# z and r gates of two of four batches by seven products over 64 partitions, two at a time on the halves of the array

## The chip, the cores and the metric

The kernel runs on one core of a Trainium2 chip. The metric is the device time of one execution in microseconds (us); of several runs the median is given. All arithmetic is float32.

## The reference, cut to what matters

Two layers work on 16 batches of 1024 nodes with 128 features; `adj` is a 1024 x 1024 matrix. The second layer takes nearly all of the time: a gated recurrent step, five times.

```
x = layernorm(x + adj @ (x @ weight) + bias)          # layer 0
h = x
for step in range(5):                                  # layer 1
    m  = adj @ h                                       # in_matrix == out_matrix == adj
    av = concat([m, m])
    u3 = h @ u3_w.T + u3_b
    z  = sigmoid(av @ w3_w.T + w3_b + u3)
    r  = sigmoid(av @ w4_w.T + w4_b + u3)
    hv = tanh(av @ w5_w.T + w5_b + (r * h) @ u5_w.T + u5_b)
    h  = (1 - z) * h + z * hv
out = layernorm(x + h)
```

Since both halves of `av` are the same, the kernel adds the two halves of w3, w4 and w5 once, at the start, and then works with 128 x 128 weights.

## The kernel before, in words

The batches go in four groups of four (`q`, 0 to 3; `QUAD` = 4), and each group makes five steps (`s`): 20 steps in the loop at L845. All instructions are written out by this Python code; the framework then orders each engine's queue by the written order and by what is ready, except that everything under `in_order` (L492, `tc.keep_in_program_order`) keeps its written order on its engine. All gate matmuls are under it, so TensorE's order in the gates is the one that the code spells out. The four engines that matter are TensorE (PE), VectorE (DVE), ScalarE (ACT) and the DMA queue of SyncE (SP).

**Adjacency products** (`aggregate`, L417). The product of adj with the state of four batches is made by a seven-product form (Winograd's) at two levels. The outer level pairs batches 0 and 1 with batches 2 and 3; `chain` (L358) makes the outer products 1 and 2, then 3, then 6 and 7, then 5 and 4, each by seven inner products in the order 1, 5, 6, 2, 7, 3, 4. The results of an inner product lie in the PSUM banks pa, pb and pc, and are emptied by ScalarE copies (L382 to L385 and L388) and VectorE additions (L386 and L387) into `first`, `rows` and `agg`. At the end L453 to L457 add the last pieces together in `agg` (features on partitions, nodes along the free axis), quarter after quarter: L455 for the second half of the nodes of each batch, L457 for the first half of batches 2 and 3. The first half of the nodes of batches 0 and 1 is ready in `agg` long before. `hooks` puts other work between inner products.

**Gates.** A unit is one batch `k` and one half `h` of its nodes (512 columns): eight units a step. A unit takes five matmuls of 128 x 128 weights on 512 columns: u3 on h (`gate_first`, L501; its result is copied by ScalarE, L509, into a second bank, so that r and z each have a seed to add to), w4 (`gate_r`, L519), w3 (`gate_z`, L534), w5 (L542) and u5 on r*h (L543). ScalarE makes the sigmoids (L522, L537) and the tanh (L553), VectorE r*h (`gate_rh`, L529) and the update in three operations: hv - h, times z, plus h (L558 to L560). The units are interleaved (L913 to L917): u3 of unit u, then w5 and u5 of unit u-3, then w4 and w3 of unit u-1. At a step's end `gates_begin` (L925) runs u3 of the next step's first three units. r of unit 0 and z of unit 0 are hooked into the last adjacency chain.

**Turning the state.** The next step needs the state with nodes on partitions. `turn_rows` (L577) transposes 32 x 32 blocks on VectorE and writes them to DRAM by an SP DMA; `fetch_rows` (L590) reads them back into `rows` with four DMAs for each batch. The first inner sums of the next step (`first_sums`, L317 to L320) are put between the updates of batch 3. In the last step of a group the state goes to `closing`, and the layernorm of a finished batch (`close`) is hooked into the adjacency chains of the next group.

**PSUM** has eight banks: a, c, g0, g1, g2 by tags, and pb and two `seeded` ones standing. `z_of` and `rh_of` are parts of `tsum`.

Of the kernel before, what the change touches and what calls it, by code (L numbers as in the profile page):

```python
# [15 lines left out]
STEPS = 5  # L16
QUAD = 4
# [3 lines left out]
def kernel(  # L21
# [62 lines left out]
    turned = [dram.tile([16, P, 64], F32, name=f"turned{i}") for i in range(3)]  # L84
# [67 lines left out]
    e12 = const.tile([P, 2, 4, 2, QT], F32, name="e12")  # L152
# [7 lines left out]
    for n in outer:  # L160
        e = extra[n]
        left[n] = {
            1: quarter(n, 0, 0), 2: quarter(n, 0, 1), 3: e[:, 2], 4: quarter(n, 1, 1),
            5: e[:, 0], 6: e[:, 1], 7: e[:, 3] if n < 3 else quarter(n, 1, 0),
        }
# [11 lines left out]
    def inner_left_12():  # L177
        a = [[blk[0][:, :, 2 * j : 2 * j + 2, ts(i, QT)] for j in range(2)] for i in range(2)]
        return left_sums(*a[0], *a[1], e12[:, :, 0], e12[:, :, 1], e12[:, :, 3], e12[:, :, 2])
# [33 lines left out]
    w_t = {n: const.tile([P, D], F32, name=f"{n}_t") for n in ("w3", "w4", "w5", "u3", "u5")}  # L213

# [16 lines left out]
    def layer1_weights():  # L231
# [5 lines left out]
        for w, raw in raw_of.values():  # L237
            if w.shape[1] == 2 * D:
                tc.keep_in_program_order(
                    nc.vector.tensor_add(raw[:, :D], raw[:, :D], raw[:, D : 2 * D])  # L240
                )

    def turn_weights():
        for name, (_, raw) in raw_of.items():
            pt = bank(f"pt_{name}")
            tc.keep_in_program_order(nc.tensor.transpose(pt[:, :P], raw[:, :D], ident))
            nc.vector.tensor_copy(w_t[name], pt[:, :P])
# [67 lines left out]
    def inner_sums(xs, dst):  # L315

        yield nc.vector.tensor_sub(dst[0], xs(0, 1), xs(0, 0))  # L317
        yield nc.vector.tensor_sub(dst[1], xs(1, 1), dst[0])
        yield nc.vector.tensor_sub(dst[2], xs(1, 1), xs(0, 1))
        yield nc.vector.tensor_sub(dst[3], xs(1, 0), dst[1])  # L320
# [96 lines left out]
    def aggregate(tag, src, hooks, turned=True):  # L417
# [34 lines left out]
        )  # L452
        for dst, a, b in ((0, p7, p4), (1, p7, p4), (2, p7, p5), (3, p7, p5)):  # L453
            cols = ts(dst % 2, HALF)
            nc.vector.tensor_add(agg[:, dst, HALF:], a[:, cols], b[:, cols])  # L455
            if dst >= 2:
# [40 lines left out]

    def gate_first(tag, u, part=None, seed=True):
        k, h = UNITS[u]
        pu = bank(f"pu_{tag}_{k}_{h}", part if part is None else part_of[part])  # L500
# [38 lines left out]
    def update_products(tag, k, h, part=None):  # L539
        cols = ts(h, HALF)  # L540
        ph = bank(f"ph_{tag}_{k}_{h}", part if part is None else part_of[part])
# [28 lines left out]

    def half_of(h):
        return (slice(None), 4) if h is None else (ts(h, HALF), 2)

    def between(k, h):
        return turned[k % 2] if h is None else turned[2][ts(h, 8)]

    def turn_rows(k, h=None, to=None):  # L577
        cols, n = half_of(h)
        to = between(k, h) if to is None else to
# [5 lines left out]
        tc.keep_in_program_order(nc.sync.dma_start(  # L585
            to.rearrange("g p x -> p g x"), t.rearrange("p (g x) -> p g x", x=64)
        ))
# [373 lines left out]
```

## Time and profile before

| what | value |
|---|---|
| median of 3 runs | 1768.44 us (1768.34 to 1768.82) |
| the profiled execution | 1769.02 us, span 1766.9 us |
| TensorE matmuls busy | 1755.7 us (99%) |
| TensorE weight loads busy | 1265.8 us (72%), beside the matmuls |
| VectorE busy | 1301.9 us (74%) |
| ScalarE busy | 800.0 us (45%) |
| one step (448.41 to 525.05 in the span) | 76.6 us |
| granted TensorE clock | 0.999 |

The profile is of one execution. A line of the page's groups or of the timeline names the source line (L519), the engine, the operation, what it writes and reads, the shape, the count, and in brackets how long the engine sat idle before it and what ended that. PEld is TensorE's weight load. A float32 matmul appears as two loads and two matmul instructions. The ends of matmuls are modelled, so their spacing is read from the starts.

### The profile page before, as it was taken

What the parts mean: (1) busy time and instruction counts of PE and PEld (TensorE: products, weight loads), DVE (VectorE), ACT (ScalarE), POOL (GpSimd) and SP (SyncE); (2) the same over time, 40 slices, a digit from 0 to 9 for tenths busy, and PEclk for the clock granted to TensorE, in tenths of its full rate; (3) what the DMA queues carried; (4) which work ended last, traced back from release to release, by engine and by line L of the source; (5) the groups of instructions that cost most, each with busy time, mean ns of one, the idle gap of its engine ahead of it and who ended that gap; (6) DMA issues with size and microseconds to landing.
All of it is one profiled execution on the core that took longest, in us unless ns stands there. A gap on an engine that the chain in (4) does not pass through costs nothing.

```text
span 1766.9 us, 19951 instructions
## 1 busy us (share of the span) xinstructions
PE 1755.7 (99%) x6709; PEld 1265.8 (72%) x6709; DVE 1301.9 (74%) x2286; ACT 800.0 (45%) x1424; POOL 103.3 (6%) x152
## 2 busy tenths in 40 slices
PE   9999999999999999999999999999999999999998
PEld 8988885766858577685867758586675857668584
DVE  7977777676766847777778667777778577777778
ACT  4355565334353434435354452535445353443537
POOL 1202220000000000000000000000000000000004
PEclk9999999999999999999999999999999999999999
DMA  8144354051423505143351424324243241514232
GB/s 276 49 143 144 120 137 107 20 119 26 94 60 72 143 12 133 46 120 68 87 131 56 112 57 99 85 71 119 55 113 99 57 93 27 131 25 107 60 84 95
DMA packets 405332, 161.34 MB, mean 91 GB/s; under 512 B 388336, under 2 KB 389488, under 8 KB 405232
## 3 DMA queue, kind: packets, MB, share of 16 engines
q1 hardware_dynamic: 402960, 153.01, 34.3%
q0 software_dynamic: 1696, 5.24, 1.1%
q10 hardware_dynamic: 576, 1.84, 0.3%
q8 instruction: 53, 0.87, 0.2%
q14 instruction: 47, 0.39, 0.1%
HBM read 93.98 MB, written 65.01 MB: 90 GB/s over the span
## 4 chain that ended last, share of the span: by engine, by line
PE 98%; DMA 1%; DVE 0%; POOL 0%; ACT 0%; issue 0%; POOLq 0%; SPq 0%; DVEq 0%; ACTq 0%
PE pb L398 25%; PE pc L398 14%; PE pa L398 14%; PE pu L519 8%; PE ph L542 8%; PE pu L501 8%; PE ph L543 8%; PE seeded L534 8%; PE pc_x L398 3%; PE pa_x L398 3%; PE seeded L475 2%; DMA hid<-in_adj_dram 1%; DMA agg<-in_adj_dram 0%; PE pt L633 0%; PE pt_end L836 0%; POOL rstd L265 0%
## 5 line engine op out<-in xcount | busy, mean ns | idle before, releaser
L398 PE MATMUL pb<-e,inner 128*128 128x256 f32 x864 | 206.2, 379 | 0.2 <-ACT pb L382 0.2
L558 DVE TENSOR_TENSOR tsum<-tsum,hid 128x512 f32<-128x512 f32 x158 | 108.7, 688 | 106.4 <-ACT tsum L553 106.3
L553 ACT ACTIVATE tsum<-ph,bh 128x512 f32<-128x512 f32 x158 | 108.5, 687 | 164.6 <-PE ph L543 164.5
L398 PEld LDWEIGHTS pb<-e,inner 128*128 128x128 f32 x864 | 167.7, 194 | 19.2 <-ACT pb L382 0.6
L519 PE MATMUL pu<-agg,w_t 128*128 128x512 f32 x320 | 163.7, 593 | 0.0
L542 PE MATMUL ph<-agg,w_t 128*128 128x512 f32 x320 | 163.4, 592 | 0.0
L543 PE MATMUL ph<-tsum,u_t 128*128 128x512 f32 x320 | 163.4, 592 | 0.0
L534 PE MATMUL seeded<-agg,w_t 128*128 128x512 f32 x320 | 163.4, 592 | 0.0
L501 PE MATMUL pu<-hid,u_t 128*128 128x512 f32 x320 | 157.0, 592 | 0.0
L522 ACT ACTIVATE tsum<-pu,br 128x512 f32<-128x512 f32 x160 | 110.1, 688 | 85.6 <-PE pu L519 85.6
L398 PE MATMUL pb<-s,inner 128*128 128x256 f32 x576 | 148.5, 380 | 0.0
L398 PE MATMUL pb<-a,inner 128*128 128x256 f32 x576 | 143.9, 379 | 0.0
L529 DVE TENSOR_TENSOR tsum<-tsum,hid 128x512 f32<-128x512 f32 x160 | 110.1, 688 | 37.9 <-ACT tsum L522 37.9
L398 PE MATMUL pc<-e,inner 128*128 128x256 f32 x560 | 133.9, 379 | 0.0
L398 PEld LDWEIGHTS pb<-s,inner 128*128 128x128 f32 x576 | 110.5, 194 | 24.8 <-issue 10.4
L537 ACT ACTIVATE tsum<-seeded,bz 128x512 f32<-128x512 f32 x160 | 110.0, 688 | 29.3 <-PE seeded L534 29.3
L398 PEld LDWEIGHTS pb<-a,inner 128*128 128x128 f32 x576 | 111.9, 194 | 12.4
L398 PEld LDWEIGHTS pc<-e,inner 128*128 128x128 f32 x560 | 109.2, 195 | 12.8 <-PE pu L501 0.7
L543 PEld LDWEIGHTS ph<-tsum,u_t 128*128 128x128 f32 x320 | 60.8, 190 | 76.5 <-issue 59.6
L542 PEld LDWEIGHTS ph<-agg,w_t 128*128 128x128 f32 x320 | 60.6, 190 | 75.1 <-issue 74.4
L501 PEld LDWEIGHTS pu<-hid,u_t 128*128 128x128 f32 x320 | 60.8, 190 | 73.5 <-issue 72.2
L559 DVE TENSOR_TENSOR tsum<-tsum 128x512 f32<-128x512 f32 x158 | 109.1, 691 | 4.9
(192 smaller groups left out, 2854.2 us busy)
## 6 DMA issues: line engine op xcount, KB each, us to landing
turned<-ypad SPq DMA_DIRECT2D x48, 512.0 KB, 3.8
rows<-turned SPq DMA_DIRECT2D x192, 128.0 KB, 2.9
hvs<-saved SPq DMA_DIRECT2D x24, 512.0 KB, 4.1
rows<-saved SPq DMA_DIRECT2D x20, 512.0 KB, 3.7
hid<-hidden SPq DMA_DIRECT2D x64, 128.0 KB, 3.4
turned<-ypad SPq DMA_DIRECT2D x32, 256.0 KB, 2.9
rows<-turned SPq DMA_DIRECT2D x128, 64.0 KB, 2.1
hidden<-ypad SPq DMA_DIRECT2D x12, 512.0 KB, 4.1
```

The costliest lines, as they stand in the source:

```text
L398: product = nc.tensor.matmul(bank_of[a][:, ts(o, QT)], chunk(a, o, c), left[n][a][:, c, :], start=(a in (1, 5) and o == 0 and c == 0), sto ...
L501: in_order(nc.tensor.matmul(pu, w_t["u3"], hid[:, k, ts(h, HALF)], start=True, stop=True, skip_group_check=True))
L519: in_order(nc.tensor.matmul(pu, w_t["w4"], agg[:, k, cols], start=False, stop=True, skip_group_check=True))
L522: pin(nc.scalar.activation(rh[:, cols], pu, AF.Sigmoid, bias=br))
L529: pin(nc.vector.tensor_mul(rh[:, cols], rh[:, cols], hid[:, k, cols]))
L534: in_order(nc.tensor.matmul(pz, w_t["w3"], agg[:, k, cols], start=False, stop=True, skip_group_check=True))
L537: pin(nc.scalar.activation(z_of[k % 2][:, cols], pz, AF.Sigmoid, bias=bz))
L542: in_order(nc.tensor.matmul(ph, w_t["w5"], agg[:, k, cols], start=True, stop=False))
L543: in_order(nc.tensor.matmul(ph, w_t["u5"], rh_of[k % 2][:, cols], start=False, stop=True))
L553: pin(nc.scalar.activation(hv, ph, AF.Tanh, bias=bh))
L558: pinned(nc.vector.tensor_sub(hv, hv, hid[:, k, cols]))
L559: pinned(nc.vector.tensor_mul(hv, hv, z_of[k % 2][:, cols]))
```

## The change

In 19 of the 20 steps (all but the very last) the gates of batches 0 and 1 are made otherwise; batches 2 and 3 keep the old form, in another order. In the 20th step everything stays.

The features of batches 0 and 1 are mixed in `rows` and `agg`: slot 0 holds the first 64 features of both batches (batch 0 on partitions 0 to 63, batch 1 on 64 to 127) and slot 1 the last 64. Weights r over z (w4 over w3) times this are a 2 x 2 block product: blocks of 128 outputs by 64 features on the left, 64 features by 512 nodes on the right. It takes seven products over 64 partitions for each batch instead of four over 128. The weights for both halves of the partitions are in the new `split`, with the four left sums made once. The four right sums are made every step (`gate_sums`), from `agg` into `first`. The products of batch 0 use partitions 0 to 63, those of batch 1 partitions 64 to 127, and they are written alternately into different banks. w5 for both batches also becomes half products, four for each half of the nodes (`carry`). u3 and u5 stay as full products: u3 for the first half of the nodes, and for the step from the first half to the second (`steps_along`).

The first new order on TensorE is: two u3 products before the inner product 3 of the last chain, two more before 4, then 1, n1 (w5 for nodes' first half), 2, 5, 6, 3, 7, n2 (w5, second half), 4, then four u5 products. After it units 4 to 7 follow. `gates_begin` at a step's end is left only where the 20th step comes next. All updates of batches 0 and 1 and both their turns come before unit 4 in the written order.

```diff
-    turned = [dram.tile([16, P, 64], F32, name=f"turned{i}") for i in range(3)]
+    turned = [dram.tile([16, P, 64], F32, name=f"turned{i}") for i in range(QUAD)]
...
+    split = const.tile([P, 9, D], F32, name="split")
+    SPLIT = {"w4": 0, "w3": 2, "w5": 4}
+    gate_left = {a: split[:, i] for a, i in {1: 0, 2: 1, 3: 8, 4: 3, 5: 6, 6: 7, 7: 2}.items()}
...
+        sums = gate_sums(0, nc.vector) if pairs else iter(())
         for dst, a, b in ((0, p7, p4), (1, p7, p4), (2, p7, p5), (3, p7, p5)):
             cols = ts(dst % 2, HALF)
             nc.vector.tensor_add(agg[:, dst, HALF:], a[:, cols], b[:, cols])
-            if dst >= 2:
+            if dst == 0:
+                next(sums, None)
+            elif dst == 1:
+                deque(sums, 0)
+            else:
                 nc.vector.tensor_add(agg[:, dst, :HALF], agg[:, dst, :HALF], p5[:, cols])
...
+    BANKS = (
+        {"pa": ("s0", "s1"), "pc": ("g0", "g1"), "pb": ("b", "c"), "ph0": ("g2", "a"),
+         "ph1": ("s0", "s1")},
+    )
...
+    def steps_along(p):
+        for e in range(2):
+            h = hid[:, 2 * p + e]
+            nc.vector.tensor_sub(steps_of_h[:, 2 * p + e], h[:, side(p, 1)], h[:, side(p, 0)])
+
+    def seed_pair(tag, p, role):
+        for e, t in enumerate(take(tag, p, role)):
+            k = 2 * p + e
+            h = hid[:, k, side(p, 0)] if role == "pa" else steps_of_h[:, k]
+            in_order(nc.tensor.matmul(
+                t, w_t["u3"], h, start=True, stop=True, skip_group_check=True
+            ))
...
+    def gate_product(tag, p, a):
+        n1, n2 = side(p, 0), side(p, 1)
+        right = {1: agg[:, 2 * p, n1], 2: agg[:, 2 * p + 1, n1], 3: agg[:, 2 * p + 1, n2]}
+        right.update({a: gate_right[p][:, i] for i, a in enumerate((5, 6, 7, 4))})
+        role = {1: "pa", 2: "pa", 5: "pc", 3: "pc"}.get(a, "pb")
+        for e in range(2):
+            at = ts(e, 64)
+            in_order(nc.tensor.matmul(
+                held[p, role][e], gate_left[a][at], right[a][at], start=False, stop=True,
+                skip_group_check=True,
+            ))
+        if a == 1:
+            take(tag, p, "pb")
+        for e in range(2):
+            pa, pb_, pc = (held[p, i][e] for i in ("pa", "pb", "pc"))
+            z, r = z_to[p][e], r_to[p][e]
+            if a == 1:
+                nc.scalar.copy(pb_, pa)
+            elif a == 5:
+                nc.scalar.copy(z[:, n2], pc)
+            elif a == 6:
+                nc.scalar.copy(r[:, n2], pb_)
+            elif a == 2:
+                nc.scalar.activation(r[:, n1], pa, AF.Sigmoid, bias=br)
+                times_h(p, e, n1)
+            elif a == 3:
+                in_order(nc.vector.tensor_add(r[:, n2], pc, r[:, n2]))
+                nc.scalar.activation(r[:, n2], r[:, n2], AF.Sigmoid, bias=br)
+            elif a == 7:
+                in_order(nc.vector.tensor_add(z[:, n2], pb_, z[:, n2]))
+                nc.scalar.activation(z[:, n2], z[:, n2], AF.Sigmoid, bias=bz)
+            else:
+                nc.scalar.activation(z[:, n1], pb_, AF.Sigmoid, bias=bz)
+        if a == 7:
+            for e in range(2):
+                times_h(p, e, n2)
+
+    def carry(tag, p, j):
+        to = take(tag, p, f"ph{j}")
+        for f in range(2):
+            for e in range(2):
+                at = ts(e, 64)
+                in_order(nc.tensor.matmul(
+                    to[e], split[at, SPLIT["w5"] + f], agg[at, 2 * p + f, side(p, j)],
+                    start=(f == 0), stop=True, skip_group_check=True,
+                ))
...
+    def update(p, j, e, put=lambda op: op):
+        cols, k = side(p, j), 2 * p + e
+        hv = rh_of[e][:, cols]
+        nc.scalar.activation(hv, held[p, f"ph{j}"][e], AF.Tanh, bias=bh)
+        put(nc.vector.tensor_sub(hv, hv, hid[:, k, cols]))
+        put(nc.vector.tensor_mul(hv, hv, z_to[p][e][:, cols]))
+        put(nc.vector.tensor_add(hid[:, k, cols], hid[:, k, cols], hv))
...
+        if paired:
+            p, e = divmod(k, 2)
+            moves = [(between(2 * p + f, h)[:, ts(e, 64)], t[ts(f, 64)]) for f in range(2)]
...
-            if q == s == 0:
-                hooks[54][3, (0,)] = [call(gates_begin, tag, 3)]
-            hooks[54][4] = [call(gate_r, 0, False)]
-            hooks[54][3, (1,)] = [call(gate_z, 0)]
-            aggregate(tag, rows, hooks, s > 0)
...
+            hooks[54][5] = [call(steps_along, 0)]
+            hooks[54][3, (0,)] = [call(seed_pair, tag, 0, "pa")]
+            hooks[54][4] = [call(seed_pair, tag, 0, "pc")]
+            aggregate(tag, rows, hooks, s > 0, True)
+            if last:
+                load_pairs(q + 1)
+            final = q == NQ - 1 and s == STEPS - 2
+            gates_of_pair(tag, 0)
+            for j in range(2):
+                reset_products(0, j)
+                for e in range(2):
+                    update(0, j, e)
+            for k in range(2):
+                if last:
+                    turn_rows(k, None, closing[k])
+                    fetch_hidden(k)
+                else:
+                    turn_rows(k, None, None, not final)
+            if not last:
+                for k in range(2):
+                    fetch_rows(k)
...
-            for u in range(3, 8):
-                gate_first(tag, u, (u - 3) % 3)
-                step_update(u - 3, (u - 2) % 3)
-                gate_r(u - 1)
-                gate_z(u - 1)
+            gate_first(tag, 4, "c")
+            gate_first(tag, 5, 2)
+            gate_r(4)
+            gate_z(4)
+            gate_first(tag, 6, 0)
+            step_update(4, 1)
+            gate_r(5)
+            gate_z(5)
+            gate_first(tag, 7, "c")
             step_update(5, 2)
+            gate_r(6)
+            gate_z(6)
             gate_r(7)
             gate_z(7)
             step_update(6, 0)
             step_update(7, 1)
-            part_of.insert(0, part_of.pop())
-            then = f"{q}_{s + 1}" if not last else f"{q + 1}_0"
-            gates_begin(then, 2 if q == NQ - 1 and s == STEPS - 2 else 3)
+            if final:
+                gates_begin(f"{q}_{s + 1}", 2)
```

Not shown are the preparation of `split` from the weights (once), two ScalarE copies that settle the room of the left sums (once), and the loads and turns that mix the features of batches 0 and 1 at a group's start.

## The prediction

> **What bounds the kernel now.** I read the page first: the engines' shares and the chain that ended last.
>
> ```profile
> PE   9999999999999999999999999999999999999998
> ...
> PEclk9999999999999999999999999999999999999999
> ...
> PE 98%; DMA 1%; DVE 0%; POOL 0%; ACT 0%; issue 0%; POOLq 0%; SPq 0%; DVEq 0%; ACTq 0%
> ```
>
> TensorE is busy in every slice at the full granted clock and is 98% of the chain. No other engine has idle TensorE time into which its delays could fall, so a wait that reaches TensorE is paid in full. Then the timeline, for the gate phase of one plain step (batches 0 to 3, step 3; it runs from 495.01, the end of the adjacency products, to 525.05; the step is 76.6 us). TensorE first:
>
> ```profile
> 501.02 1.02 PE L501 MATMUL pu<-hid,u_t 128*128 128x512 f32 x2
> 501.87 1.02 PE L542 MATMUL ph<-agg,w_t 128*128 128x512 f32 x2
> 502.73 1.02 PE L543 MATMUL ph<-tsum,u_t 128*128 128x512 f32 x2
> 503.59 1.02 PE L519 MATMUL pu<-agg,w_t 128*128 128x512 f32 x2
> ```
>
> One float32 matmul over 512 columns is two instructions (x2). The starts are 0.86 us apart, so a matmul costs 0.86 (a "slot") and each of its two passes 0.43; the shown 1.02 has the modelled tail. The next view is VectorE (DVE) in the same stretch, and the one weight load that waited for it:
>
> ```profile
> 500.22 0.69 DVE L558 TENSOR_TENSOR tsum<-tsum,hid 128x512 f32<-128x512 f32 x1 [1.22 <-ACT tsum L553]
> ...
> 500.95 0.69 DVE L559 TENSOR_TENSOR tsum<-tsum 128x512 f32<-128x512 f32 x1
> ...
> 501.56 0.69 DVE L529 TENSOR_TENSOR tsum<-tsum,hid 128x512 f32<-128x512 f32 x1
> ...
> 502.16 0.68 DVE L560 TENSOR_TENSOR hid<-hid,tsum 128x512 f32<-128x512 f32 x1
> ...
> 502.31 0.19 PEld L543 LDWEIGHTS ph<-tsum,u_t 128*128 128x128 f32 x1 [0.24 <-DVE tsum L529]
> ...
> 507.17 1.25 DVE L581 STREAM_TRANSPOSE ypad<-hid 128x1024 f32<-128x1024 f32 x1
> ```
>
> Three readings. An operation on 512 columns takes a DVE step of 0.60 us, or 0.72 where it needs the one just before (500.22 to 500.95). The reset product of unit 2 waits for r*h of L529, which ended at 502.25; its load followed 0.06 later, and the matmul was due at 502.73: DVE is just 0.2 us ahead of TensorE here. And r*h was put between L559 and L560, ahead of an operation written earlier: free operations fill the gaps, otherwise the written order holds. Last, engines by stretch:
>
> ```profile
> 448.41:495.01 46.60, 46.60 (x208) 40.32 (x207) 30.46 (x43) 13.67 (x25) 0.00 (x0) 1.00 0.30 68
> 495.01:525.05 30.04, 30.04 (x72) 13.30 (x71) 23.25 (x34) 17.88 (x28) 0.00 (x0) 1.00 0.31 71
> ```
>
> In the gate phase (second line; columns PE, PEld, DVE, ACT) DVE is busy 23.25 of 30.04 us, 77%.
>
> **What the Trainium skill says.** "TensorE: Matmul & The Clock Gate", Part 3: products over fewer partitions gain only by running at the same time in different row groups; four such tiles [...] gave 3.07 times; matmuls start and end in program order. No row here shows a tiled matmul. The same page, Part 2 (LDWEIGHTS): a load's time follows the columns, not the rows; so a half product needs a whole load. The loads here are 0.19, two per 0.43 pass: they fit. "TensorEngine Tiling (Array Packing)", Key Properties: a change of tiling mode drains TensorE; not shown here. Its Performance Considerations: tiling does not speed up emptying PSUM; that is where my sum ends.
>
> **The change, part by part** (per step; 19 of 20 steps have it).
>
> *TensorE's work.* Units 0 to 3 cost 20 slots: u3, w4, w3, w5, u5 four times. After: 4 slots of u3 (pa, pc), 22 half products (7 x 2 and w5's 8), 4 slots of u5. If two halves run at once, the 22 are 11 slots: 19 in all, -0.86. Passes start in order, and both passes of a product use the same half. So the first half product's pass 1 runs alone, its pass 2 beside the other's pass 1, and so on: half a slot is lost at the ends, +0.43. Two mode changes: bounds 0 and 0.35 each (0.16, the tail that 592 ns shows over 430, plus a load of 0.19 no longer hidden); I take 0.1 each, +0.2.
>
> *VectorE's work.* r*h (4) and the updates (12) stay. Added are 4 gate sums, 2 steps along h, 2 adds for r, 2 for z: 10 x 0.60 = 6.0 us. The 2 steps along h fall into the idle stretch before L386 (4.47 us), free; bounds 0 and 0.3. The other 8 fall in the gate phase: 23.25 + 4.8 = 28 of some 30 us. ScalarE: 6 copies for 4 seeds, 2 x 0.6 more on 17.9 busy of 30; it matters only by order.
>
> *Walk through the pair*, 0 being the end of the adjacency products (495.01 above). From L388's end at -0.1 DVE has 11 operations that come first as written: dst 0 to 3 of L455 and L457 (6), L387 (1), gate sums (4). At 0.60 each with small gaps it is free at 6.8 (before: without the sums, 498.32, or 3.3). TensorE: product 1, n1 and 2 to 3.87, 5 to 4.73, 6 to 5.58 (second half); their sums are ready at 1.9 and 3.7, in time. ScalarE (0.20 after the product; 0.69 a sigmoid, 0.59 a copy): r of product 2 to 5.02, copies of 5 to 5.61 and 6.20, of 6 to 6.79 and 7.38. Product 3 writes the banks of 5, so its halves start at 5.86 and 6.45 (0.25 for semaphore and load) instead of 5.15; product 7 writes those of 6: 7.04 and 7.63. n2 ends at 9.8. DVE: r*h 6.8 to 8.0, r adds to 9.2, z adds end 9.9 and 10.5. Product 4 needs those banks: 10.15 and 10.75, end 11.6. The r, z and w5 of four units were 12 slots, 10.3. With the mode changes: **+1.5**.
>
> *Then unit 4.* Four reset products from 11.8; the first tanh is done at 13.55 (0.86+0.20+0.69). DVE, idle by then, has 12 update operations, then two transposes, and r*h of unit 4 is written after all of them. By the rule of gap filling: 11 update operations and the first transpose (6.7+1.2), the last addition (0.6), and in the gap behind it r*h: 22.05 to 22.74, and unit 4's u5 product starts at 23.0. TensorE arrives after 4 resets and 6 more products (u3 of 4, 5, 6; w4, w3, w5 of 4) at 11.8 + 8.6 = 20.4. **+2.6.** Queued behind on TensorE are the other 13 products, the rest of the step. Bounds: 0 if r*h goes as soon as its sigmoid is ready (18.7); 3.8 if both transposes go first.
>
> *Moved.* The three u3 products at a step's end (2.58 us, 525.05) go; they covered the turn of batch 3. In the new order unit 6's tanh ends 0.83 before the step does; the inner sums 1 and 2 end 2.7 and 6.2 after it, needed at 3.3 and 6.7: 0, at most 1.0 if DVE is late. Turns of batches 0 and 1 issue two DMAs each instead of one and move behind each other on SP; writes 3.9 us, then eight fetch issues of 0.48, landing 2.9: by 32.6, against the first inner sum at 34.2. Covered by 1.6 us; behind it on SP only batches 2 and 3 wait. POOL gets nothing in the steps. Weights, settling and pair loads happen a few times: under 1 us.
>
> *Sum:* 1.5 + 2.6 = 4.1 us a step, x 19 = 78 us. On the profiled execution's 1769.0 (span 1766.9 and 2.1 around it) that is 1847; the median of the runs is 0.6 lower: **1846 us**. Own range 1822 (product stalls half as long, no mode cost) to 1880.
>
> **Rivals.** (1) *The saved slot is seen* (other side): DVE keeps up, because the late dst additions are put behind the z adds and r*h of unit 4 ahead of the updates. Then -0.86 + 0.43 + 0.1 = -0.33 a step: 1762; without the skew of half a slot 1754. For it: DVE idles 7 of 30 us. Against: 20 us of DVE work stand ahead of unit 4's product as written, and TensorE needs 18.5 to get there; it decides for faster where the stalls left are under 0.3 us a step. (2) *Only the products stall*, r*h of unit 4 goes when ready: 1.5 x 19 = 28, 1797. (3) *Both transposes first*: 5.3 x 19, 1870. (4) *The halves do not run at once*: 22 slots for 11, stalls behind them hidden but for unit 4's: (18.9 - 10.3 + 0.2 + 2.6) x 19 = 217, 1985. Against it is the skill's 3.07. (5) Gain and stalls cancel: within 3.5 us.
>
> **Chances.** Forecast 0.40, (2) 0.14, (3) 0.12, (4) 0.06: slower 0.72. (1) 0.20: faster. (5) 0.08: same (within 0.2%, about what a measurement of this kernel can tell from no change). The range 1758 to 1885 leaves out (4), half of (1) and a few hundredths above.
>
> **What would show it.** Half products' passes of one pair starting together, 11 pairs in some 9.9 us: right; 0.43 apart in single file: (4). Weight loads of products 3 and 4 waiting for ScalarE's copies and DVE's z adds, 0.4 to 0.7 each: the first term. A wait of over 2 us once a step at L543's counterpart of unit 4, released by r*h, DVE full before it: the second. DVE with gaps of 1 us before those waits would prove me wrong; TensorE still at 99% with a step under 76.6 would prove (1).

## The result and the profile after

The changed kernel takes **1888.24 us** (median of 4 runs, 1886.84 to 1888.62) beside 1768.39 (1768.13 to 1768.82) for the kernel before: a ratio of 1.0676, 95% interval 1.0658 to 1.0695. It is 120 us slower, where 78 were forecast; the time lies 3 us above the range. The profiled execution took 1888.17 us with a span of 1886.0 (before: 1766.9). First the page of the changed kernel: engines, slices, granted clock, chain, and the one group that is new among the idle times.

```profile
PE 1816.3 (96%) x7092; PEld 1280.5 (68%) x7092; DVE 1404.3 (74%) x2492; ACT 804.9 (43%) x1464; POOL 102.0 (5%) x152
...
PE   8999999999999999999999999999999999999998
...
PEclk9999999999999999999999999999999999999999
...
PE 83%; DVE 10%; ACT 3%; DMA 2%; issue 2%; POOL 0%; SPq 0%; DVEq 0%; POOLq 0%; ACTq 0%
...
L582 PE MATMUL ph<-tsum,u_t 128*128 128x512 f32 x168 | 95.9, 655 | 34.1 <-DVE tsum L568 34.1
```

TensorE falls from 98% of the chain to 83%, and VectorE comes to 10%. The slices hide two things: TensorE is busy for 1816 us with less work than before (1756), and a mean granted clock of 0.980 (before 0.999) is still printed as a row of nines. L582 is u5 on r*h, the counterpart of L543; L568 is r*h. The waits of TensorE, next (total, times, longest):

```profile
PE ph L582 <- DVE tsum L568: 34.1, 16, 2.1
PE pb L666 <- DVE tsum L688: 13.9, 5, 4.2
PE pb L427 <- ACT pb L411: 3.8, 1, 3.8
```

Three places, then: one wait of 2.1 us in 16 of the 19 steps, some long ones at the pair's product 4 (L688 are the z adds), and one in an adjacency chain (L427), which turns out to be in the opening. By stage, E being the start of the first matmul after the adjacency products, or of the first half product (before: 265.10 in the first step, 1644.56 in the 19th, a step 76.64; after: 273.26 and 1757.09). The 19th gate phase holds the two u3 products at its end:

| stage | before | after | more | forecast |
|---|---|---|---|---|
| opening, to E of the first step | 265.1 | 273.3 | 8.2 | under 1 |
| 15 steps that end no group | 1149.6 | 1229.6 | 80.0 | 61.5 |
| 3 steps that end a group | 229.9 | 254.2 | 24.3 | 12.3 |
| 19th gate phase | 31.8 | 38.1 | 6.3 | 4.1 |
| last step and end | 90.6 | 90.8 | 0.2 | 0 |

**A plain step** takes 82.02 us (group 1, step 2, E = 849.26): 11.27 to the first u5 product, 3.54 for the four u5 products, and then this on TensorE:

```profile
868.49 1.02 PE L581 MATMUL ph<-agg,w_t 128*128 128x512 f32 x2
871.64 1.78 PE L582 MATMUL ph<-tsum,u_t 128*128 128x512 f32 x2 [2.13 <-DVE tsum L568]
873.21 1.91 PE L558 MATMUL pu<-agg,w_t 128*128 128x512 f32 x2
874.92 1.26 PE L573 MATMUL seeded<-agg,w_t 128*128 128x512 f32 x2
876.01 1.02 PE L540 MATMUL pu<-hid,u_t 128*128 128x512 f32 x2
```

u5 of unit 4 was due 0.86 after 868.49, at 869.35, and starts at 871.64: 2.29 us late. And then the starts stand 1.57, 1.71 and 1.09 apart instead of 0.86. The view by stretch says why (columns: length, PE, PEld, DVE, ACT and POOL busy, granted clock, DMA share, GB/s):

```profile
860.00:869.30 9.30, 9.30 (x23) 3.63 (x20) 7.48 (x14) 7.19 (x12) 0.00 (x0) 1.00 0.01 2
871.60:876.00 4.40, 4.36 (x6) 1.84 (x7) 2.64 (x4) 1.37 (x2) 0.00 (x0) 0.61 0.93 194
876.00:885.40 9.40, 9.40 (x23) 4.19 (x22) 6.89 (x11) 5.38 (x8) 0.00 (x0) 1.00 0.72 155
```

A clock of 0.61 over 4.40 us is half speed for (1 - 0.61) x 2 x 4.40 = 3.4 us, and costs 1.7. This happens in 13 of the 16 steps with that wait. What TensorE waited for, in VectorE's timeline:

```profile
868.57 0.68 DVE L725 TENSOR_TENSOR tsum<-tsum 128x512 f32<-128x512 f32 x1
869.17 1.24 DVE L737 STREAM_TRANSPOSE ypad<-hid 128x1024 f32<-128x1024 f32 x1
870.33 0.65 DVE L726 TENSOR_TENSOR hid<-hid,tsum 128x512 f32<-128x512 f32 x1
870.90 0.68 DVE L568 TENSOR_TENSOR tsum<-tsum,hid 128x512 f32<-128x512 f32 x1
871.50 1.24 DVE L737 STREAM_TRANSPOSE ypad<-hid 128x1024 f32<-128x1024 f32 x1
```

Eleven update operations without a gap (the last is shown), the first transpose, the last addition, r*h, the second transpose: the order that the prediction gave.

**A step that ends a group** takes 84.6 to 84.9. In the second one VectorE stands still in the middle of the pair:

```profile
1020.13 1.28 DVE L657 TENSOR_TENSOR tsum<-tsum,hid 128x512 f32<-128x512 f32 x2
1023.89 0.69 DVE L346 TENSOR_TENSOR inner<-rows 128x512 f32<-128x512 f32 x1 [2.47 <-issue]
1024.50 0.68 DVE L685 TENSOR_TENSOR tsum<-pc,tsum 128x512 f32<-128x512 f32 x1
```

L346 is an inner sum of the *next* group's first step. It stands ahead of the r adds (L685) and waits for the new group's state, a transfer that SP issued at 1019.30; the chain of waits has it as follows.

```profile
1019.30 3.46 DMA rows<-saved
```

TensorE's product 4 waits until 1027.04 (3.90 us idle), and the pair takes 16.3 us.

**The opening.** ScalarE, and TensorE behind it, in the changed kernel:

```profile
31.90 1.14 ACT L184 COPY a<-hvs 128x512 f32<-128x512 f32 x2 [7.48 <-DMA a<-a]
32.95 0.58 ACT L417 COPY first<-pb 128x512 f32<-128x512 f32 x1
33.56 0.36 ACT L411 COPY pb<-pa_x 128x256 f32<-128x256 f32 x1
```

```profile
29.10 1.03 PE L427 MATMUL pc_x<-e,inner 128*128 128x256 f32 x4
33.97 2.07 PE L427 MATMUL pb<-e,inner 128*128 128x256 f32 x4 [3.84 <-ACT pb L411]
35.83 1.91 PE L427 MATMUL pa_x<-s,rows 128*128 128x256 f32 x4
37.54 1.81 PE L427 MATMUL pb<-s,inner 128*128 128x256 f32 x4
39.19 1.03 PE L427 MATMUL pc_x<-e,rows 128*128 128x256 f32 x4
```

L184 is in `settle_left_12`, the two copies that bring a left sum into the place of an outer block once that block is no longer needed. They wait for a GpSimd transfer that reads the block. ScalarE takes its work in order, so the copy that TensorE needs (L411) stands behind them: 3.84 us idle, and again slow products after it (5.2 us for the three from 33.97 to 39.19, where 0.86 each is usual).

### The profile page after: what moved, and what is told of

It reads as the page before. It is cut to its first block, busy times and chain, and to the rows that moved or that the text cites. A ratio compares the mean times of both kernels' runs of the same rounds, so it can differ in the third digit from the quotient of the medians.

```text
span 1886.0 us, 21009 instructions
## 1 busy us (share of the span) xinstructions
PE 1816.3 (96%) x7092; PEld 1280.5 (68%) x7092; DVE 1404.3 (74%) x2492; ACT 804.9 (43%) x1464; POOL 102.0 (5%) x152
## 3 DMA queue, kind: packets, MB, share of 16 engines
q1 hardware_dynamic: 418928, 153.01, 33.3%
q10 hardware_dynamic: 576, 1.84, 0.3%
## 4 chain that ended last, share of the span: by engine, by line
PE 83%; DVE 10%; ACT 3%; DMA 2%; issue 2%; POOL 0%; SPq 0%; DVEq 0%; POOLq 0%; ACTq 0%
PE pb L427 23%; PE pa L427 12%; PE pc L427 12%; PE ph L582 4%; PE pu L558 4%; PE seeded L573 3%; PE ph L581 3%; PE pb L666 3%; PE pa_x L427 2%; PE pc_x L427 2%; DVE tsum L725 2%; DVE tsum L724 2%; DVE hid L726 2%; PE seeded L651 2%; PE pc L651 2%; PE seeded L666 2%
## 5 line engine op out<-in xcount | busy, mean ns | idle before, releaser
L427 PE MATMUL pb<-a,inner 128*128 128x256 f32 x760 | 187.4, 379 | 0.0
L427 PE MATMUL pb<-e,inner 128*128 128x256 f32 x672 | 162.0, 381 | 5.9 <-ACT pb L411 3.8
L427 PEld LDWEIGHTS pb<-a,inner 128*128 128x128 f32 x760 | 147.2, 194 | 16.8
L427 PE MATMUL pb<-s,inner 128*128 128x256 f32 x576 | 149.4, 382 | 1.0 <-DVE agg L415 0.8
L427 PEld LDWEIGHTS pb<-e,inner 128*128 128x128 f32 x672 | 130.7, 195 | 21.9 <-ACT pb L411 4.2
L485 DVE TENSOR_TENSOR agg<-rows 128x512 f32<-128x512 f32 x88 | 58.4, 686 | 114.7 <-ACT rows L417 114.7
L427 PE MATMUL pc<-e,inner 128*128 128x256 f32 x560 | 133.9, 379 | 0.0
L582 PE MATMUL ph<-tsum,u_t 128*128 128x512 f32 x168 | 95.9, 655 | 34.1 <-DVE tsum L568 34.1
L427 PEld LDWEIGHTS pb<-s,inner 128*128 128x128 f32 x576 | 111.0, 195 | 25.0 <-issue 9.5
L427 PEld LDWEIGHTS pc<-e,inner 128*128 128x128 f32 x560 | 109.2, 195 | 12.8 <-issue 1.4
L597 DVE TENSOR_TENSOR tsum<-tsum,hid 128x512 f32<-128x512 f32 x82 | 56.5, 689 | 66.2 <-ACT tsum L592 65.2
L558 PE MATMUL pu<-agg,w_t 128*128 128x512 f32 x168 | 99.3, 676 | 0.1
L666 PE MATMUL pb<-first,split 64*128 64x512 f32 x228 | 85.4, 649 | 13.9 <-DVE tsum L688 13.9
L737 DVE STREAM_TRANSPOSE ypad<-hid 128x1024 f32<-128x1024 f32 (+1 forms) x92 | 97.3, 1057 | 1.7
L573 PE MATMUL seeded<-agg,w_t 128*128 128x512 f32 x168 | 89.2, 613 | 0.0
L581 PE MATMUL ph<-agg,w_t 128*128 128x512 f32 x168 | 85.8, 592 | 0.0
L582 PEld LDWEIGHTS ph<-tsum,u_t 128*128 128x128 f32 x168 | 30.9, 194 | 79.3 <-DVE tsum L568 54.9
L427 PE MATMUL pa<-s,tsum 128*128 128x256 f32 x320 | 84.7, 379 | 0.0
L540 PE MATMUL pu<-hid,u_t 128*128 128x512 f32 x168 | 82.2, 593 | 0.0
```

Of the source, the lines that this page charges most:

```text
L427: product = nc.tensor.matmul(bank_of[a][:, ts(o, QT)], chunk(a, o, c), left[n][a][:, c, :], start=(a in (1, 5) and o == 0 and c == 0), sto ...
L540: in_order(nc.tensor.matmul(pu, w_t["u3"], hid[:, k, ts(h, HALF)], start=True, stop=True, skip_group_check=True))
L558: in_order(nc.tensor.matmul(pu, w_t["w4"], agg[:, k, cols], start=False, stop=True, skip_group_check=True))
L573: in_order(nc.tensor.matmul(pz, w_t["w3"], agg[:, k, cols], start=False, stop=True, skip_group_check=True))
L581: in_order(nc.tensor.matmul(ph, w_t["w5"], agg[:, k, cols], start=True, stop=False))
L582: in_order(nc.tensor.matmul(ph, w_t["u5"], rh_of[k % 2][:, cols], start=False, stop=True))
```

## The experiments

The theory to be tested (letter B in the expectations): the order of VectorE's queue sets the stall at unit 4, the idle time halves TensorE's clock, and what is made faster there is in part given back at the next chain, where the state of batches 0 and 1 comes back late. Against it stand that the half products do not run two at a time, and (C) that VectorE simply has too much work. All runs stand beside 1768.2 to 1768.4 us of the kernel before. A time without a range is that of a single run; what it shows is then read from its trace, step by step.

### Both halves on the same rows (e1_same_half)

```diff
-            at = ts(e, 64)
+            at = ts(0, 64)
...
-                at = ts(e, 64)
+                at = ts(0, 64)
```

Both batches' half products use partitions 0 to 63; batch 1's gates are then made from batch 0's features, and the amount of work is the same.

> Both half products of a pair read partitions 0 to 63 (weights and data), so they share one half of the array and cannot run beside each other; batch 1's gates are thus made from batch 0's features, all else is as in the changed kernel. If the pairs of the changed kernel really ran at once, 22 half products now take 22 slots of 0.86, so the stretch from the first half product to the first reset product goes from 11.3 to about 19 us in a plain step; the waits for ScalarE and VectorE inside it vanish; the step goes from 82.0 to about 89.5 and the kernel to about 2030 us. If the pairs had run in single file all along, nothing changes: 1888 us.

Measured: 2006.4 us. The pair takes 19.08 in every step, where 22 half products in single file are 22 x 0.86 = 18.9. First the changed kernel, then this one:

```profile
518.64 1.13 PE L666 MATMUL seeded<-agg,split 64*128 64x512 f32 x4
519.60 1.88 PE L701 MATMUL ph<-agg,split 64*128 64x512 f32 x8
521.32 1.02 PE L666 MATMUL seeded<-agg,split 64*128 64x512 f32 x4
522.18 1.02 PE L666 MATMUL pc<-first,split 64*128 64x512 f32 x4
```

```profile
538.96 1.98 PE L666 MATMUL seeded<-agg,split 64*128 64x512 f32 x4
540.78 3.59 PE L701 MATMUL ph<-agg,split 64*128 64x512 f32 x8
544.21 1.88 PE L666 MATMUL seeded<-agg,split 64*128 64x512 f32 x4
```

x4 is two half products of two passes each: 0.86 us apart on the two halves, 1.72 on one. Half products do run at once, which is worth 7.8 us a step in the pair; rival (4) is out. The kernel is 118 us slower and not 142, in part since behind 12 of its 16 waits at unit 4 the slow products are missing.

### Filling the wait (e2_fill)

```diff
-            step_update(4, 1)
             gate_r(5)
             gate_z(5)
             gate_first(tag, 7, "c")
+            step_update(4, 1)
```

> r and z of unit 5 and u3 of unit 7 are put ahead of unit 4's update on TensorE: 2.6 us of useful work before the product that waited 2.3 us. Theory A (my forecast and nothing more: the written order on VectorE makes the wait): the wait goes, and with it the half clock behind it: 82.0 to about 78 us a plain step, the kernel to about 1830 us. Theory B (the fetch of the turned batches 0 and 1 is next in line: it lands 34.5 us after the last adjacency product, whatever TensorE does): the wait goes, but the next step's third inner product waits some 3 us for the inner sums instead; a plain step takes 81.4 as the one step without the half clock does, the kernel about 1880 us. Theory C (VectorE simply has too much to do): the wait moves to unit 5's reset product.

Measured: 1872.65 us. The wait at unit 4 is gone and so are the slow products behind it (units 4 to 7 take 17.29 instead of 21.38, mean clock 0.992), but of the 15 plain steps twelve still take 80.7 to 81.4 and three 81.9 to 82.5, and the next chains grow from 45.83 to some 49. TensorE's waits of this kernel:

```profile
PE pc L427 <- DVE inner L346: 16.5, 15, 1.5
...
PE pb L427 <- DVE inner L347: 10.3, 7, 1.5
```

Of 4.1 us that the wait and its slow products took, 3.2 come back at the first inner sums (L346, L347) of the next chain. (The second of these waits stands in all 15 steps, 1.47 us each, and ends 0.15 us after the sum L347; for eight of them the profile names ScalarE.) The stall had been their cover.

### The turn later (e3_turn_later)

The turns and fetches of batches 0 and 1 are moved from their place to just behind `gate_z(4)`.

> The transposes of batches 0 and 1 are written after r*h of unit 4. On VectorE r*h then comes 1.8 us sooner and the first transpose 1.2 us later. Theory A: the wait at unit 4 falls from 2.3 to 0.5 us, too short for the half clock: a plain step 78.5, the kernel about 1837 us. Theory B: the fetch lands 1.2 us later, so the saving comes back as a wait in the next step's third inner product: a plain step 82.0 to 82.6, the kernel 1885 to 1897 us.

Measured: 1894.87 us. u5 of unit 4 waits only 0.56, and no slow products stand behind it in any step, but the chains take 49.0 to 50.3. The same time is lost further on, with a little more.

### TensorE kept busy (e4_busy_wait)

```diff
+        if part == 1 and k == 2:
+            idle = ps_m.tile([P, HALF], F32, tag="a", name=f"idle_{tag}")
+            for _ in range(2):
+                in_order(nc.tensor.matmul(idle, w_t["u3"], hid[:, 2, cols], start=True, stop=True))
```

Two products that nobody reads stand between w5 and u5 of unit 4.

> Two more u3 products (1.7 us), whose result nobody reads, go ahead of the product that waits, so TensorE idles 0.6 us there instead of 2.3. If the half clock behind the wait comes from idling, the granted clock stays at 1.00 in every step and unit 4's reset products and the four after them keep 0.86 us: 1.7 us a plain step less. By theory B 0.65 of that reaches the step (81.4, kernel about 1880 us), by theory A all of it (80.3, about 1866 us). If the slow passes come from something else, the kernel stays at 1888 us or grows.

Measured: 1880.53 us, 7.7 less. **The 15 plain steps take 81.3 us on average instead of 82.0, with 1.7 us more work in each.** Of the rest, the 19th gate phase is 1.7 shorter, the three steps that end a group, which have no such wait to fill, are 2.4 longer each, and the opening is 3.1 shorter, which is not the edit's doing: its long wait was not followed by half clock this time.

```profile
866.09 1.88 PE L585 MATMUL idle<-hid,u_t 128*128 128x512 f32 x4
868.38 1.13 PE L586 MATMUL ph<-tsum,u_t 128*128 128x512 f32 x2 [0.41 <-DVE tsum L568]
869.35 1.02 PE L558 MATMUL pu<-agg,w_t 128*128 128x512 f32 x2
```

Behind the 0.41 us the products stand 0.86 to 0.97 apart: in no step does half clock follow this wait. So the slow products come from TensorE's idle time and not from what they read. Units 4 to 7 take 19.69 instead of 21.38; on average 1.0 of this gain is again lost at the next chain (46.1 to 47.5, where 45.83 was usual).

### The next group's sums kept behind (e5_sums_pinned)

```diff
-                    sums_of(rows, (1, 2))
-                    sums_of(rows, (3,))
+                    sums_of(rows, (1, 2), True)
+                    sums_of(rows, (3,), True)
```

> The inner sums of the next group, made in the last step of a group, keep their written order on VectorE behind the gates of the pair (before, they stood ahead of the r adds and z adds, though they wait for a load). Theory: the load's wait (2.5 us on VectorE, then 3.9 us on TensorE at product 4, then the half clock) goes in the three steps that end a group: about 84.7 to 82 us each, the kernel about 1880 us. If the wait comes from the loads alone, it stays at 1888 us.

Measured: 1867.75 us. The three steps that end a group fall from 84.7 to 79.4, 5.3 each or 16 in all, twice what was expected, for these steps have no wait at unit 4 that could come in its place; the pair takes 11.27 there as elsewhere. The other 4.5 us are the opening (1.1), the plain steps (1.5) and the 19th gate phase (1.7): only 10 of the 16 waits at unit 4 were followed by half clock, where 13 were before.

### Without the gate sums (e6_no_sums)

The four right sums are not made; the products 5, 6, 7 and 4 take pieces of `agg` instead, so r and z are others.

> The four right sums of the gates are left out: products 5, 6, 7 and 4 read pieces of agg as they are (the gates' values are others). VectorE has 2.4 us less to do ahead of the pair. My theory (the wait at unit 4 is a chain that starts with the first tanh, on a VectorE that was idle before): the z adds come in time, the stretch from the first half product to the first reset product falls from 11.3 to about 10.5 us, the wait at unit 4 stays 2.3 us: 0.8 us a step, the kernel about 1873 us. Theory C (VectorE has too much to do): the wait at unit 4 shrinks or goes as well, and with it the half clock: 1810 to 1840 us.

Measured: 1874.92 us. The pair falls from 11.27 to 10.62, the wait at unit 4 stays at 2.29. With 2.4 us less VectorE work ahead of the pair the wait does not move: it is the order of what is written ahead of r*h, not the amount of work (C is out for this wait).

### Taking the rest away: six versions

Each of these starts from the changed kernel with the edit of e2_fill. **e7_fill_halves** turns and fetches the pair by halves of the nodes, the first half ahead of the second half's updates:

```diff
+    def turn_half(h, final):
+        for k in range(2):
+            turn_rows(k, h, None, not final)
+        for k in range(2):
+            fetch_rows(k, h)
```

> The order of e2_fill, and batches 0 and 1 are turned and fetched by halves of the nodes, the first half ahead of the second half's updates. If the fetch is what e2_fill ran into, it now lands about 4 us sooner, and a plain step is 11.3 + 3.5 + 5.3 + 12.1 + 45.8 = 78.0 us: the kernel about 1820 us (the steps that end a group keep their 8 us). If the rival holds, that 24 small transfers cost SP and the DMA engines as much as 12, it stays at e2_fill's 1873 us.

Measured: 1879.59, slower than e2_fill. SP issues 24 small transfers instead of 12, some 0.47 us for a fetch and 0.7 for a write, in order, each group of fetches behind the landing of its writes, and has issued the last fetch at E + 32.9 (E + 31.2 in e2_fill); the chain takes 49.2 to 50.4. Expected 1820: missed.

**e8_all** adds e5's edit and writes the last additions in `agg` behind the pair, and the first sigmoids behind the copies.

> e7_fill_halves and e5_sums_pinned together, and two changes inside the pair: the additions of dst 2 and 3 are written behind the pair's z adds, and the r sigmoids of product 2 behind the copies of products 5 and 6 on ScalarE. By my theory products 3 and 4 then hardly wait: about 10.2 us for the stretch instead of 11.3, a plain step 77.0 us, the kernel about 1785 us. It does not come below 1768 us unless the half slot at the ends and the mode changes cost less than the saved slot, which leaves at most 0.2 us a step.

Measured: 1860.52 (expected 1785): the pair stays at 11.27, because the framework orders what is not under `in_order` by readiness, and put the sigmoids and additions where they were. Steps that end a group take 78.3, plain ones 81.2 to 82.8.

**e9_pool_fetch** puts those instructions under `in_order` and has the first half fetched by GpSimd's queue.

> e8_all, and the pair's copies, sigmoids, r adds, z adds and r*h in a fixed order (copies of products 5 and 6 ahead of the sigmoids of product 2; r adds and z adds ahead of r*h), and the first node half of batches 0 and 1 is fetched by POOL's queue, so that SP can write the second half without waiting. If SP's one queue is what e7_fill_halves and e8_all ran into (16 fetches of 0.47 us to issue, in order, each group behind its landing), the fetch lands some 3.5 us sooner and a plain step is about 77.5 us: the kernel about 1790 us. If POOL's transfers start later than SP's would, or the DMA engines are the limit, it stays at e8_all's 1860 us. The pair's stretch: 10.4 us, from 11.3.

Measured: 1832.56 (1831.84 to 1834.54), ratio 1.0364, 1.0348 to 1.0379; 1790 was expected. The pair takes 10.63, but the first inner sum still starts only at E + 33.3 (E = 832.74), and the second 3.5 us behind it, with unit 6's update between:

```profile
864.20 1.89 PE L427 MATMUL pa<-a,rows 128*128 128x256 f32 x8
866.86 1.97 PE L427 MATMUL pc<-e,inner 128*128 128x256 f32 x8 [0.77 <-DVE inner L346]
870.30 1.97 PE L427 MATMUL pb<-e,inner 128*128 128x256 f32 x8 [1.47 <-ACT hvs L304]
```

(For the last wait the profile names ScalarE; the sum L347 was made at 869.50, so it is that which came last.)

**e13_two_sums** puts the second sum directly behind the first, and tries to move the opening's copies.

> The best version so far (1832.6 us) with the copies of the opening moved as well, and with the second of the four inner sums put directly behind the first, ahead of unit 6's update (in it, product 6 of the next chain waited 1.64 us for that sum, which stood 3.5 us behind the first). If the order of the two sums is the cause of that wait: 1.64 less in each of 15 steps and 6.3 at the start, 1832.6 - 24.6 - 6.3 = 1802. Rival, the second sum has to wait for its own transfer, or the updates put back by 0.6 us make batches 2 and 3 late for their products: 1815 to 1827.

Measured: 1840.4, slower than e9_pool_fetch and above both forecasts. Product 6 no longer waits, product 7 does, for the third sum (L348), which now has the updates of both units ahead of it:

```profile
877.76 1.97 PE L427 MATMUL pb<-a,inner 128*128 128x256 f32 x8 [1.58 <-DVE inner L348]
```

The order of the sums is not the cause; the wait moves on through them. VectorE has some 8 us of work from the landing (869.9) to the last sum, and TensorE, whose three u3 products no longer stand in between, wants it sooner.

**e10_fill_pinned** is e2_fill and e5_sums_pinned together.

> e2_fill and e5_sums_pinned together. The two act in different steps: e2_fill is 15.6 us under the changed kernel with the group-ending steps unchanged, and e5_sums_pinned takes 5 us off each of three steps, so about 1857 us. It stays far above the kernel before, since the fetch of batches 0 and 1 still sets the step (80.9 us).

Measured: 1852.49 (1851.65 to 1853.95), ratio 1.0475, 1.0457 to 1.0492. The two gains add up: 15.6 and 20.5 alone, 35.8 together.

**e11_no_fetch** is e2_fill without the fetches of batches 0 and 1, so that the next step works on what `rows` holds.

> e2_fill without the fetches of batches 0 and 1 between the steps of a group: the next step's adjacency products then work on what rows holds, so the output is another. If the fetch is what sets e2_fill's step, the waits in the next step's second and third inner product (1.4 and 1.6 us) go: a plain step 77.9 to 78.1 us, the kernel about 1828 us. If those waits come from VectorE's updates instead, it stays at 1873 us.

Measured: 1839.14. Plain steps take 78.88 instead of 81.0, chains 46.78 instead of some 49. So the fetch is 2.1 us of each step, the next bound behind the stall at unit 4. The 0.9 us above the expected 78.0 are a wait for ScalarE's copy (L412), 0.68 us in 14 steps, by a part of product 3 that the framework pulled ahead of product 6.

### The opening's copies (e12_settle_later, e14_settle_pool)

In the first the two copies and the weights' load are written one chain later.

> In the changed kernel the two copies that bring the left sums of products 1 and 2 to their place (settle_left_12) stand on ScalarE between two copies of the opening's second chain and wait for a GpSimd transfer that lands at 31.8 us; TensorE waits 3.84 us behind them, and the four products after that take 5.2 us for 3.4 to 3.6. Here the two copies, and the load of the gate weights that needs their room, are moved to the third chain of that phase, after the transfer. Read as cause: the opening is 6.3 us shorter, the first half product starts at 267.0 instead of 273.3, and everything after it is as before: 1888.2 - 6.3 = 1882. Rival, the opening waits for the transfers of the data at its own pace and another wait takes the place: 1887 to 1889.

Measured: 1886.11 us (1884.50 to 1888.93). The copies still went out at 31.75, at the same place; the first half product stands at 273.66. As a test of the opening it shows nothing. In the second GpSimd makes the copies, and they are written behind its transfers:

```diff
-            nc.scalar.copy(quarter(n, 1, 0), left[n][7])
+            nc.gpsimd.tensor_copy(quarter(n, 1, 0), left[n][7])
```

> In the run before, the two copies were written later but still went out on ScalarE at 31.75 us, ahead of the second chain's copies, so that it tested nothing. Here the changed kernel's two copies are made by GpSimd, behind its transfers, and ScalarE has nothing there that waits for the transfer. Read as cause: no wait of 3.8 us at 33.8 and no slow products after it, the first half product starts at 267.0 instead of 273.3 to 273.7, and the time is 6.3 lower, 1880 to 1882. Rival, the opening's next wait takes its place (the weights' load, behind the copies, or GpSimd's own): first half product at 271 or later and 1885 to 1888.

Measured: 1882.08 us (1880.91 to 1883.57), ratio 1.0640, 1.0623 to 1.0658. E of the first step is 267.03: 6.2 less.

```profile
30.64 1.13 PE L427 MATMUL pb<-e,inner 128*128 128x256 f32 x4 [0.20 <-ACT pb L411]
```

Two copies in the wrong queue cost 6.2 us, 3.8 of idle time and the rest in slow products. The other 2.0 us by which the opening is longer than before stay open.

No version comes near the kernel before; the best is e9_pool_fetch, 64 us above it.

## Why the prediction was right in sign and short in size

*Half products, and the half slot at the ends (+0.43).* Two at a time is right, as "TensorE: Matmul & The Clock Gate", Part 3, of the Trainium skill had it, and e1_same_half shows it. The half slot is wrong. In the changed kernel the two halves of the first pair start together:

```profile
849.26 0.70 PE L666 MATMUL seeded<-agg,split 64*128 64x512 f32 x2
```

These two passes start 0.007 us apart, the next two as well, and so on to the first stall; until then no pass runs alone. Each of the two mode changes costs 0.2 us, where 0.1 was taken: the first pair of passes starts 0.10 later behind the last full product than usual, and the next passes another 0.10 later behind it; on the way back it is the same.

*Product stalls, +1.5.* Right in kind: weight loads of product 3 wait for ScalarE's copies (L678, 38 times in 19 steps), those of product 4 for the z adds (L688, 34 times). Too large in size: 11.27 against 10.31 is +0.97. In the step shown above products 3, 7 and 4 start at 5.53, 6.50 and 9.63 where 5.86, 7.04 and 10.15 were worked out, so the half slot that is not there makes up most of the difference. The stalls are VectorE's work in the pair: without the gate sums it takes 10.62, with the late additions and the sigmoids put behind 10.63.

*Unit 4's wait, +2.6.* Right, 2.29, in the order foretold. It is shown by e2_fill and e3_turn_later (another order, no or little wait) and by e6_no_sums (less work, same wait).

*"... a wait that reaches TensorE is paid in full."* **Here the prediction failed first.** A wait was paid with its length and 1.7 us more, since it halved the clock of what came next. "TensorE: Matmul & The Clock Gate", Part 1, of the Trainium skill has this: the clock is set by the activity in a free-running window of 3413 ns. The traces agree. A stretch at half clock behind a wait lasts 3.41 us, or twice that, and all of a run start on one grid of such windows (295.12, 377.04 and 458.96 in the changed kernel are 24 windows of 3.413 apart). The page's words for the loss, a whole idle window, do not fit: part of one is enough. Here are a window with the wait of the step shown above and the next one, then the same for a step without half clock (columns as above):

```profile
868.56:871.97 3.41, 1.28 (x4) 0.42 (x3) 3.41 (x6) 0.57 (x1) 0.00 (x0) 1.00 0.07 15
871.97:875.39 3.42, 3.42 (x5) 1.35 (x4) 1.95 (x3) 0.92 (x2) 0.00 (x0) 0.50 0.96 199
537.47:540.88 3.41, 1.42 (x4) 0.35 (x2) 3.41 (x5) 1.00 (x2) 0.00 (x0) 1.00 0.00 0
540.88:544.30 3.42, 3.28 (x8) 1.61 (x9) 2.60 (x5) 1.77 (x3) 0.00 (x0) 1.00 0.90 192
```

TensorE idles 2.13 of the 3.41 us in the first window, and the clock is halved in the next. In the third the same wait is cut by the border: 1.99 us fall into it, and the clock stays. Of the 16 waits, the 13 that left 2.03 to 2.13 us idle in one window were followed by half clock, and the three that left 1.84, 1.85 and 1.99 were not. Over all traces of this case, every one of 118 windows at full clock with at least 2.01 us idle was followed by half clock, and of 258 with 0.9 to 2.01 us only four were. So where a wait falls on the grid decides: in e1_same_half the same 2.13 us stand in 16 steps and only 4 were followed, and a wait of 3.03 us in the opening of e4_busy_wait, cut in two halves, was not. I had read the mean clock of before (0.999) as a property of the kernel; it was a property of its having no gap.

*The fetch, "covered by 1.6 us".* **Wrong.** The prediction had it land at E + 32.6. The changed kernel, in a step without half clock (group 0, step 3, E = 518.64), has this on SP, and then on VectorE:

```profile
539.82 3.73 SPq L748 DMA_DIRECT2D turned<-ypad  x4
545.90 4.03 SPq L757 DMA_DIRECT2D rows<-turned  x8
```

```profile
553.28 0.69 DVE L346 TENSOR_TENSOR inner<-rows 128x512 f32<-128x512 f32 x1 [1.61 <-DMA rows<-turned]
```

The writes are issued from E + 21.2 to 24.9. SP then stands for 2.35 us until they have landed, and only then come eight fetches; the first inner sum starts at E + 34.6. From the first write to the first fetch this is 6.1 us, where the sum had 3.9 for the writes; in the kernel before that is what one write takes until its fetch (508.44 to 512.31), and here there are four. Where unit 4's stall and the half clock (4.2 us late together) hold TensorE up, this is hidden; where they do not, it is the next bound (e2_fill, e11_no_fetch). That is why filling the wait gave 15 us and not 78. Its root is in the layout: each slot of `rows` holds halves of both batches, so no fetch can start until both are updated and turned, while the kernel before fetches batch 0 some 8.5 us ahead of batch 1.

*"Weights, settling and pair loads happen a few times: under 1 us."* **Wrong, by the most in proportion.** Settling cost 6.2 us (e14_settle_pool), since its copies waited in ScalarE's order ahead of work that TensorE needed. The pair loads cost 5.3 in each of three steps (e5_sums_pinned), since sums that need the new group's state were put ahead of the r adds. I had counted their work, which is small, and not the queue that they stand in, a check which I made for SP alone.

*The sum.* For the 15 plain steps the terms of the prediction come to 0.97 + 0.22 (the four u5 products and the six products after them) + 2.29 + 0.1 (the chains) = 3.6 each, 54 in all, where 61.5 were forecast. Half clock in 12 of them adds 12 x 1.7 = 20; a late fetch after each of the other three 0.9 to 1.0, together 3; the first steps of two groups have a pair of 12.40, together 2, since VectorE makes a transpose for the next group there ahead of the r adds (L767, 1.25 us, at 692.60 and 1106.21): 79 of the 80.0 measured. The steps that end a group, the opening and the 19th gate phase (half clock too) give the other 39. So the terms that I priced were 8 us too high in the plain steps, and what I did not price came to some 50. That the range was missed by only 3 us is in part luck: the half slot, 8 us in 19 steps, does not exist and stood in for terms that do.

*Rival (1), the saved slot is seen:* nowhere. Even e9_pool_fetch, where neither the pair's long stalls nor unit 4's are left, has mostly steps of 79.6 to 80.4 beside 76.64, and its three steps that end a group, which have no turned state to fetch, take 77.70.

*A reading of the lines.* The load at 502.31, which the prediction takes for unit 2's and for waiting, belongs to unit 1, whose r*h (498.32) had long ended; the r*h that ends at 502.25 is unit 2's. The loads before and behind it (501.88 and 502.73) come with the same 0.24 us of idle time. So these lines do not show that VectorE was 0.2 us ahead; the sum does not use it.

**What stays open:** why the clock was halved behind four windows with less than 2.01 us idle (0.92, 0.93 and twice 1.92); the last 2 us of the opening; and whether this layout can be fetched in time at all, which no version here achieved.

## What to carry to other kernels

Where the bound engine has no gaps, price a new wait by its length and by what comes after it: here a TensorE wait of 2.3 us cost 4.0 in 13 of 16 cases, and two useless products in it were better than the wait. Of everything that is moved or added, ask whose queue it stands in and what is behind it there, also for copies that run once: two copies cost 6 us, the next group's sums 16. And before taking away work at the end of a stage, look for the transfer that it covers, and take a layout that ties two transfers together as a delay of the first one.

## What the runs showed of the hardware

- Half products of 64 partitions on the two halves run at once in float32: 22 take 11.27 us with stalls, 19.08 in single file. Each change between full products and half ones cost 0.2 us.
- The two halves of a pair start 0.007 us apart, and the stream loses no half product at its start.
- TensorE's clock was halved for one or two windows of 3.413 us behind every window of this grid in which it had idled 2.01 us or more (118 of 118 in the 16 traces), and behind four of 258 with 0.9 to 2.01 us. The price of one such window is 1.7 us.
- GpSimd took 3.00 us for the two copies of 512 columns for which ScalarE took 1.14; there it cost nothing, since nobody waited.
